# Six side tiles an l instead of three in a recommender kernel that gathers 200 x 16384 embedding rows

## Chip, core and metric

The kernel runs on one core of one Trainium2 chip. The metric is the device time of one execution in microseconds. Times are medians of runs; one further execution was taken with the hardware profiler, and all rows below are from it. Engines are named as in the profile: PE (matrix products; PEld is its loading of weights), DVE (vector), ACT (activations), POOL (GpSimd, here only the issuer of gathers) and SP (here only an issuer of copies). "SPq" and "ACTq" are the queues of instructions of these two engines that issue copies.

## What is computed

An attention unit over a history of L = 200 items for each of B = 16384 users, then a small head. Embeddings have D = 64 numbers (256 bytes a row).

```python
h = i_emb[hist]                                  # (200, 16384, 64)
itb = jnp.broadcast_to(it[None], h.shape)        # it = i_emb[item]
feat = jnp.concatenate([h, itb, h - itb, h * itb], axis=-1)
a = dice(feat @ au_W1 + au_b1, au_alpha, axis=1) # mean and variance over the 16384 users
w = a @ au_W2 + au_b2
cur = jnp.sum(w * h, axis=0)                     # sum over the history
z = jnp.concatenate([u, it, c, cur], axis=-1)    # u = u_emb[user], c = c_emb[cate]
z = dice(z @ W1 + b1, alpha1, axis=0)
z = dice(z @ W2 + b2, alpha2, axis=0)
return z @ W3 + b3
```

`dice(x)` normalizes x over the batch, takes a sigmoid p of it and gives x * (p + alpha * (1 - p)). Nearly all the work is in the rows `h`: 200 x 16384 of them, each read from a table in memory at a place that the input names.

## The kernel before

**Steps.** The 16384 users are 128 tiles of 128 rows (NT = 128). They are worked on in ND = 8 chunks c of TD = 16 tiles. One step k is one chunk of one l: k = 8 l + c, so an l is 8 steps and the whole history is 1600. A Python loop lays the steps out (`steps`); 90 l (LPB) are the body of a loop on the chip, and the last 20 l stand behind it. The order of instructions on each engine is that of the program text; every engine runs its own in order and waits for semaphores.

**Software pipeline of a step** (`step`, L435 on). In step k: `fetch(k)` lets POOL gather the rows of chunk k into `rows[k % 5]`; `hidden(k-2)` on ACT copies the products of chunk k-2 from `px` to `xs` with a bias; `ask_hist` issues row copies on SP (queue 0) and on ACT (queue 1); `gate(k-9)` is the sigmoid on ACT; ACT then issues what is left of its share; on DVE and PE `place(k-1)` and `turn(k-1)` bring chunk k-1 into the transposed layout and multiply it into `ph` and `px`; `measure(k-2)` gathers statistics; `product(k-1)` adds the last term to `px`; `weights(k-9)` and `weigh(k-9)` form the weighted sum of a chunk nine steps back into `curT`. Where chunk k-2 is the last of an l (k % 8 = 1), `measure` and `moments` come ahead of the rest, since the gates of that l need its mean and variance; in the program they stand directly behind `hidden`.

**Two ways to fetch rows.** Most tiles are gathered: POOL issues one indirect DMA for a tile of 128 rows (`gather`, L123), with indices that `load_hist_ids` put into `idx`. Some tiles are fetched *by address*: `SIDES` (L27) names the chunks whose last tile (n = 15) is such a side tile, NS = len(SIDES) of them an l. `fetch` leaves that tile out (`TD - has_side(k)`). Its rows are copied one by one, 256 bytes each, by plain DMAs on SP and ACT (`row_by_address`, L290). For this the indices of the NS x 128 side rows of an l are loaded onto one partition (`load_addresses`, by SP, two steps into the l before), multiplied by the row size on DVE (`scale_addresses`, two steps later), and loaded in groups into registers of the issuing engine (L326, the TENSOR_LOAD of the trace); each row is then one DMA with a register in its address (L294).

**Shares.** `ask_hist(k, queue, some)` asks in step c of an l for the c-th eighth of its side rows: NS x 128 / 8 = 48 rows. `shares` gives SP the first half of these and ACT the second (SPLIT = 0.5), and cuts each half into as few equal groups as hold at most LOAD = 28 rows, one load of addresses each: here one group of 24 rows on each queue. SP issues all its groups in a step at one place; ACT issues its first group ahead of the gate and any further groups behind it (`slice(0, 1)` and `slice(1, None)`).

**Side buffers.** Side tile m (counted over all l) is collected in `side[m % 6]` (BUFS = 6) and counted by the semaphore `landed[m % 6]`. In step k, `place(k-1)` has DVE wait for all 128 rows of the tile of chunk k-1, clear the semaphore and copy the tile into `rows` (L392). A buffer's next rows are asked for once that copy is done.

The head at the end gathers the user rows in the same way, with the side tiles of chunks 3 and 5 by address and the others by `side_ids` on POOL (L669 on).

Of the kernel before, what the change touches and what calls it, by code (L numbers as in the profile page):

```python
# [23 lines left out]
LAG = 9  # L24
XR = 8
IDX = 3
SIDES = (3, 5, 7)  # L27
BUFS = 6
LOAD = 28
SPLIT = 0.5  # L30
# [5 lines left out]
def din_kernel(  # L36
# [33 lines left out]
    ZB = Z1 - ZA  # L70
    NS = len(SIDES)
    serial = iter(range(10**6))
# [18 lines left out]
    def column(c, n):  # L91
        if c in SIDES and n == TD - 1:
            return NC + SIDES.index(c)
        return c * TD + n - sum(s < c for s in SIDES)

# [185 lines left out]
    def tiles_by_address(l):  # L281

        return l * NS, range(NS)
# [71 lines left out]
    def has_side(k):  # L355
        return k % ND in SIDES

# [26 lines left out]
    def place(k):  # L384
        if has_side(k):
            l, c = divmod(k, ND)
            first, tiles = tiles_by_address(l)
            place_tile(k, first + tiles.index(SIDES.index(c)))

    def place_tile(k, m):  # L390
        await_rows(m)
        nc.vector.tensor_copy(rows[k % ROWS][:, TD - 1], side[m % BUFS])  # L392
# [271 lines left out]
    with tc.manual_schedule():  # L664
# [1 line left out]
        U = addr[(L - BODY) % 3]  # L666
        first = -(-tiles_by_address(L - BODY)[0] // BUFS) * BUFS

        tiles = [SIDES.index(c) for c in (3, 5) if c in SIDES]  # L669
        weighed = {*range(-LAG, K - LAG), K, K + 1}  # L670
        for j in range(ND + 1):
            c = j - 1
# [128 lines left out]
```

## Time and profile before

| | us |
|---|---|
| median of 3 runs | 31650.93 |
| lowest to highest | 31650.28 to 31652.98 |
| the profiled execution | 31646.96 |
| its span, first to last instruction | 31645.1 |
| busy: POOL, PE, DVE, ACT | 23853.6, 20823.3, 15548.7, 3817.4 |

How to read it: busy time leaves out instructions that only an engine's sequencer runs, and the issue of plain DMAs is one of these, so SP has no busy time at all and ACT's contains its activations alone. Groups are given as "out<-in" with their count, busy time and mean, and behind the bar the time that the engine stood idle just before them and what ended it; "issue" there means that nothing the profile shows was waited for. In a timeline the columns are start, duration, engine, line, operation, and in brackets the idle time before it; rows on SPq and ACTq are issues of copies, merged where they follow one another. The granted clock of PE was 0.806 in this execution.

### The profile page before, as it was taken

What the parts mean: (1) busy time and instruction counts of PE and PEld (TensorE: products, weight loads), DVE (VectorE), ACT (ScalarE), POOL (GpSimd) and SP (SyncE); (2) the same over time, 40 slices, a digit from 0 to 9 for tenths busy, and PEclk for the clock granted to TensorE, in tenths of its full rate; (3) what the DMA queues carried; (4) which work ended last, traced back from release to release, by engine and by line L of the source; (5) the groups of instructions that cost most, each with busy time, mean ns of one, the idle gap of its engine ahead of it and who ended that gap; (6) DMA issues with size and microseconds to landing.
All of it is one profiled execution on the core that took longest, in us unless ns stands there. A gap on an engine that the chain in (4) does not pass through costs nothing.

```text
span 31645.1 us, 223489 instructions
## 1 busy us (share of the span) xinstructions
PE 20823.3 (66%) x39536; PEld 8584.9 (27%) x39536; DVE 15548.7 (49%) x21275; ACT 3817.4 (12%) x3322; POOL 23853.6 (75%) x25259
## 2 busy tenths in 40 slices
PE   6666666666666666666666666666666666666666
PEld 2222222222222222222222222222222222222222
DVE  5444444444444444444444444444444444444445
ACT  1111111111111111111111111111111111111111
POOL 7777777777777777777777777777777777777776
PEclk8888788887888888888788888887878788887888
DMA  2111111111111111111111111111111111111111
GB/s 44 28 28 28 28 28 28 28 28 28 28 28 28 28 28 28 28 28 28 28 28 28 28 28 28 28 28 28 28 28 28 28 28 28 28 28 28 28 28 30
DMA packets 1008142, 894.16 MB, mean 28 GB/s; under 512 B 597358, under 2 KB 597559, under 8 KB 1006695
## 3 DMA queue, kind: packets, MB, share of 16 engines
q0 software_dynamic: 808128, 829.14, 15.0%
q1 hardware_dynamic: 114362, 27.92, 0.4%
q10 hardware_dynamic: 84205, 22.70, 0.3%
q14 instruction: 1136, 9.31, 0.1%
q8 instruction: 311, 5.10, 0.1%
HBM read 873.48 MB, written 4.39 MB: 28 GB/s over the span
## 4 chain that ended last, share of the span: by engine, by line
POOL 30%; issue 11%; PE 6%; DMA 5%; DVE 2%; DVEq 0%; ACT 0%; POOLq 0%; ACTq 0%
POOL rows L124 30%; DMA rows<-in_L_rec_i_emb,idx 5%; PE px L154 3%; PE ph L154 2%; PE wb L154 2%; DVE hT L149 1%; DVE wb L373 1%; DVE curT L374 0%; DVE st L382 0%; DVEq L149 0%; DVE mv L418 0%; DVE rows L392 0%; DVE addrs L141 0%; POOLq L124 0%; PE pg L154 0%
## 5 line engine op out<-in xcount | busy, mean ns | idle before, releaser
L124 POOL DMA_INDIRECT rows<-in_L_rec_i_emb,idx x25000 | 23591.6, 944 | 7633.1 <-issue 7166.6
L154 PE MATMUL ph<-hT,unit 128*128 128x512 f32 x6404 | 5969.6, 1088 | 10697.5 <-DVE hT L149 10697.5
L373 DVE SCALAR_TENSOR_TENSOR wb<-wb,au_bias,hT 128x1024 f32<-128x1024 f32 x1609 | 2079.7, 1293 | 10748.4 <-PE wb L154 10748.4
L149 DVE STREAM_TRANSPOSE hT<-rows 64x512 f32<-64x512 f32 x6404 | 4518.5, 706 | 2971.8 <-DMA rows<-in_L_rec_i_emb,idx 2529.3
L154 PEld LDWEIGHTS ph<-hT,unit 128*128 128x128 f32 x6404 | 1796.1, 311 | 13756.3 <-DVE hT L149 13561.4
L154 PE MATMUL px<-hT,blk_h 128*128 128x512 f32 x6404 | 4065.3, 723 | 0.0
L377 ACT ACTIVATE xs<-px,au_bias 128x1024 f32<-128x1024 f32 x1602 | 1784.1, 1114 | 14492.6 <-PE wb L154 14492.5
L366 ACT ACTIVATE pg<-xs,sh,rs 128x1024 f32<-128x1024 f32 x1609 | 1943.3, 1208 | 12967.9 <-issue 10092.6
L154 PE MATMUL px<-itT,blk_i 128*128 128x512 f32 x6404 | 3382.0, 610 | 0.0
L154 PE MATMUL wb<-y,blk_p 128*128 128x512 f32 x6436 | 3291.1, 593 | 11.3 <-DVE y L369 11.3
L154 PE MATMUL wb<-xs,blk_x 128*128 128x512 f32 x6436 | 3289.2, 593 | 2.6 <-DVE curT L374 2.6
L154 PE MATMUL px<-hm,blk_m 128*128 128x512 f32 x6408 | 3011.3, 592 | 0.0
L412 DVE TENSOR_TENSOR hm<-ph,itT 128x1024 f32<-128x1024 f32 x1601 | 1960.4, 1224 | 1934.9 <-PE ph L154 1934.9
L154 PEld LDWEIGHTS px<-hT,blk_h 128*128 128x128 f32 x6404 | 1627.8, 254 | 2406.1 <-issue 2304.8
L382 DVE BATCH_NORM_STATS2 st<-xs 128x6 f32<-128x512 f32 x3204 | 2058.4, 684 | 44.5 <-ACT pg L366 0.3
L369 DVE TENSOR_TENSOR y<-pg,xs 128x1024 f32<-128x1024 f32 x1609 | 1955.7, 1215 | 85.0 <-ACT pg L366 82.9
L374 DVE TENSOR_TENSOR curT<-wb,curT 128x1024 f32<-128x1024 f32 x1609 | 1969.8, 1224 | 54.8
L154 PEld LDWEIGHTS px<-itT,blk_i 128*128 128x128 f32 x6404 | 1404.8, 219 | 2000.0 <-issue 2000.0
L154 PEld LDWEIGHTS wb<-y,blk_p 128*128 128x128 f32 x6436 | 1224.5, 190 | 1551.8 <-issue 1537.2
L154 PEld LDWEIGHTS wb<-xs,blk_x 128*128 128x128 f32 x6436 | 1224.3, 190 | 1541.4 <-issue 1538.0
L154 PEld LDWEIGHTS px<-hm,blk_m 128*128 128x128 f32 x6408 | 1219.0, 190 | 1531.4 <-issue 1524.2
L124 POOL DMA_INDIRECT rows<-in_L_rec_i_emb,ids x125 | 139.7, 1118 | 39.6 <-issue 37.2
(180 smaller groups left out, 1779.3 us busy)
## 6 DMA issues: line engine op xcount, KB each, us to landing
side<-in_L_rec_i_emb SPq DMA_DIRECT2D x38400, 0.2 KB
side<-in_L_rec_i_emb ACTq DMA_DIRECT2D x38400, 0.2 KB
rows<-in_L_rec_i_emb,idx POOLq DMA_INDIRECT x25000, 2.5
idx<-in_r_hist SPq DMA_DIRECT2D x200, 62.5 KB
hT<-cs ACTq DMA_DIRECT2D x16, 500.0 KB
ucT<-catT SPq DMA_DIRECT2D x8, 512.0 KB
side<-in_L_rec_u_emb SPq DMA_DIRECT2D x256, 0.2 KB
addrs<-in_r_hist SPq DMA_DIRECT2D x200, 1.5 KB
```

What stands on the lines that cost most here:

```text
L124: nc.gpsimd.indirect_dma_start(out=dst[:, n, :], out_offset=None, in_=table, in_offset=bass.IndirectOffsetOnAxis(ap=ids, axis=0),)
L149: nc.vector.transpose(by_tile(dst[ts(e, D)], i)[:, n], of[ts(i, D), n, ts(e, S)])
L154: nc.tensor.matmul(dst[:, ts(i, CH)], lhsT, rhs[:, ts(i, CH)], start=(first and j == 0), stop=(last and j == len(pairs) - 1), skip_group_c ...
L366: nc.scalar.activation(pg, xs[k % XR], AF.Sigmoid, bias=shifts[i], scale=rstds[i])
L369: nc.vector.tensor_mul(y, pg, xs[k % XR])
L373: nc.vector.scalar_tensor_tensor(wb, wb, au_bias2, hT[k % LAG], ALU.add, ALU.mult)
L374: nc.vector.tensor_add(curT[k % ND], wb, curT[k % ND])
L377: nc.scalar.activation(xs[k % XR], px, AF.Identity, bias=au_bias)
L382: nc.vector.bn_stats(stats[l % 3][:, 2 * c + i, :], xs[k % XR][:, ts(i, CH)])
L412: nc.vector.tensor_mul(hm, ph, itT[k % ND])
```

## The change

`SIDES` names six chunks in place of three. NS is 6, so an l has 122 gathered tiles and 6 side tiles (before: 125 and 3), 768 side rows instead of 384, and 96 of them a step. Each queue's share of a step is 48 rows; LOAD stays 28, so `shares` cuts it into two groups of 24. SP issues both at its place in the step, ACT one ahead of the gate and one behind it. The six side buffers hold one l instead of two. All tensors whose width is NS or NC change with it: `idx` and `ids` have 122 columns, `side_ids` 6, `addrs` 768 addresses for each of its three l.

```diff
-SIDES = (3, 5, 7)
+SIDES = (1, 3, 4, 5, 6, 7)
...
-        tiles = [SIDES.index(c) for c in (3, 5) if c in SIDES]
+        tiles = [SIDES.index(c) for c in (3, 5)]
```

The second edit gives the places of chunks 3 and 5 among the side tiles of the users: 0 and 1 before, 1 and 3 after. The head still fetches these two tiles by address and all other user tiles by POOL.

## The prediction

> **What bounds the kernel now.** I read the page first: engine shares, then the costliest groups.
>
> ```profile
> span 31645.1 us, 223489 instructions
> PE 20823.3 (66%) x39536; PEld 8584.9 (27%) x39536; DVE 15548.7 (49%) x21275; ACT 3817.4 (12%) x3322; POOL 23853.6 (75%) x25259
> L124 POOL DMA_INDIRECT rows<-in_L_rec_i_emb,idx x25000 | 23591.6, 944 | 7633.1 <-issue 7166.6
> side<-in_L_rec_i_emb SPq DMA_DIRECT2D x38400, 0.2 KB
> side<-in_L_rec_i_emb ACTq DMA_DIRECT2D x38400, 0.2 KB
> ```
>
> No engine is full by its busy share, but POOL's gathers fill the span together with the gap in front of each: (23591.6 + 7633.1) / 25000 = 1.249 us a gather, 125 gathers an l, 156.1 us an l, 200 l = 31225 of 31645 us. The rest is some 250 gathers of items and users and the head after them. The last two rows are what moves: 76800 row copies, half on SP, half on ACT. ACT's 12% leaves them out, because an issue isn't counted as busy.
>
> Then the waits, where 1.249 is confirmed and ACT's real load shows:
>
> ```profile
> ACT xs L377 <- PE wb L154: 14492.5, 1599, 15.7
> ACT pg L366 <- issue: 10092.6, 1242, 9.0
> POOL rows L124 <- issue: 7241.2, 23739, 0.3
> ACT pg L366 <- DVE sh L180: 1629.6, 201, 8.5
> DVE hT L149 <- DMA rows<-in_L_rec_i_emb,idx: 2529.3, 1181, 5.0
> ```
>
> POOL's gap is 0.3 us every time and waits for nothing: POOL runs without a stop. DVE waits for gathered rows 2529.3 us in all (12.6 an l), so the rest of the pipeline has spare time. The row of `pg` is the important one: before the gate, ACT is "idle" 10092.6 / 1242 = 8.13 us, each time "issue". That isn't spare time, it is the row copies being issued. The real spare time of ACT is the wait of `xs`, 14492.5 us.
>
> The timeline of ACT over one l shows how a step is built (hidden, 24 rows, gate, wait):
>
> ```profile
> 15032.23 1.11 ACT L377 ACTIVATE xs<-px,au_bias 128x1024 f32<-128x1024 f32 x1 [9.28 <-PE wb L154]
> 15033.94 7.31 ACTq L294 DMA_DIRECT2D side<-in_L_rec_i_emb  x24
> 15041.38 1.21 ACT L366 ACTIVATE pg<-xs,sh,rs 128x1024 f32<-128x1024 f32 x1 [8.04 <-DVE sh L180]
> 15055.80 1.11 ACT L377 ACTIVATE xs<-px,au_bias 128x1024 f32<-128x1024 f32 x1 [13.22 <-PE wb L154]
> 15057.54 7.29 ACTq L294 DMA_DIRECT2D side<-in_L_rec_i_emb  x24
> 15064.88 1.21 ACT L366 ACTIVATE pg<-xs,sh,rs 128x1024 f32<-128x1024 f32 x1 [7.96 <-issue]
> 15073.11 1.11 ACT L377 ACTIVATE xs<-px,au_bias 128x1024 f32<-128x1024 f32 x1 [7.03 <-PE wb L154]
> ...
> 15131.03 1.11 ACT L377 ACTIVATE xs<-px,au_bias 128x1024 f32<-128x1024 f32 x1 [9.97 <-PE wb L154]
> ...
> 15140.12 1.21 ACT L366 ACTIVATE pg<-xs,sh,rs 128x1024 f32<-128x1024 f32 x1 [7.97 <-issue]
> 15149.11 1.11 ACT L377 ACTIVATE xs<-px,au_bias 128x1024 f32<-128x1024 f32 x1 [7.79 <-PE wb L154]
> ...
> 15158.50 1.21 ACT L366 ACTIVATE pg<-xs,sh,rs 128x1024 f32<-128x1024 f32 x1 [8.27 <-issue]
> ```
>
> From the start of hidden to the start of the gate it is 9.08 us (15064.88 - 15055.80) to 9.39 us (15158.50 - 15149.11): 1.7 us until the first row, in which the 24 addresses are loaded while the activation runs, then 24 rows at 0.305 us. Call this a batch; its mean is 1.11 + 8.13 = 9.24 us by the row of the waits.
>
> **The change part by part.**
>
> *Removed:* three gathers an l on POOL, 600 x 1.249 = 749 us. POOL alone then needs 122 x 1.249 = 152.4 us an l, and the run 31647 - 749 = 30898 us. (The sum is made against the profiled execution, 31646.96 us, 4 us or 0.01% under the median of the three runs, 31650.93.)
>
> *Added on ACT:* a second batch of 24 rows in every step, behind the gate. It starts as the first does, with a load of addresses beside an activation (1.21 us instead of 1.11), so I price it like the first. Its ends in the rows above are 9.08 and 9.39; the mean, 9.24, includes the long stretches in which SP issues nothing (its waits are quoted below), and those go away. I take 9.30, a little above the mean, and keep 9.08 and 9.39 for the range. Next to be late is the next hidden, queued behind the second batch on ACT, and through it PE's px. So a step on ACT takes at least 2 x 9.30 = 18.60 us; the wait of `xs` hides the second batch only while steps are longer than that, and POOL's new mean step is 152.4 / 8 = 19.05. That would fit, were it not for one step of each l:
>
> ```profile
> 15188.89 1.11 ACT L377 ACTIVATE xs<-px,au_bias 128x1024 f32<-128x1024 f32 x1 [8.79 <-PE wb L154]
> 15210.87 1.11 ACT L377 ACTIVATE xs<-px,au_bias 128x1024 f32<-128x1024 f32 x1 [11.70 <-PE wb L154]
> ...
> 15500.21 1.11 ACT L377 ACTIVATE xs<-px,au_bias 128x1024 f32<-128x1024 f32 x1 [7.49 <-PE wb L154]
> 15523.62 1.11 ACT L377 ACTIVATE xs<-px,au_bias 128x1024 f32<-128x1024 f32 x1 [13.02 <-PE wb L154]
> ```
>
> The moments of an l are worked out on DVE between hidden and the next transposes, and PE's products come after these. So this step can't be shorter than it is: 15055.80 - 15032.23 = 23.57, 21.98 and 23.41 us here, mean 22.99. Today the following step catches up (15073.11 - 15055.80 = 17.3 us); with 18.60 us of ACT work it can't. ACT's shortest l is 22.99 + 7 x 18.60 = 153.2 us, against POOL's 152.4. ACT then sets the pace, by a little: 200 x (156.1 - 153.2) = 580 us saved, 31647 - 580 = 31067; I say 31060.
>
> The Trainium skill, page "DMA: Bandwidth & Descriptors", section "Issuing engines are not separate DMA queues", says that starting DMAs on several engines saves only the time of the sequencer that starts them, "usually small relative to the DMA itself". By that rule ACT's second batch would be nearly free and the time POOL's 30898; the 7.31 us for 24 copies of 256 B speak against it here.
>
> *Added on SP:* as much again.
>
> ```profile
> SPq L326 <- DVE rows L392: 15047.6, 198, 84.3
> SPq L132 <- DMA rows<-in_L_rec_i_emb,idx: 1283.4, 449, 8.0
> 15114.66 50.55 SPq L294 DMA_DIRECT2D side<-in_L_rec_i_emb  x139
> 15018.24 0.37 SPq L132 DMA_DIRECT2D idx<-in_r_hist  x1
> ```
>
> At full pace 139 rows with their loads of addresses take 50.55 us, so the 48 rows of a step take 48 x 50.55 / 139 = 17.5, an l 140 us, and the copies of `idx` and addresses (0.37 and the like) some 1 us more. That is below 152.4. SP stands still half the time, since it is up to two l ahead and waits for side tiles to be copied out (15047.6 us); the change spends that lead (six buffers then hold one l), not the path.
>
> *Added on DVE, and the small rest:*
>
> ```profile
> L392 DVE COPY rows<-side 128x64 f32<-128x64 f32 x603 | 128.1, 212 | 12.0 <-PEq L580 4.9 <-DMA rows<-in_L_rec_i_emb,idx 3.0
> L141 DVE TENSOR_SCALAR addrs<-addrs 1x384 int32<-1x384 int32 x201 | 75.1, 374 | 4.2
> ```
>
> Three copies more an l (0.21 each, plus a wait and a clear of the semaphore) and a scaling of 768 instead of 384 addresses (at most 0.37 more): about 1 us an l, hidden in DVE's 12.6 us of waiting for rows; without that cover it is 200 us. Head and end get some nine small copies, 0 to 5 us at 0.37 an issue. I take 0.
>
> **The wait on the last side tile.** Rows of the tile of c = 7 are asked for up to the end of step 7, now behind that step's gate, and DVE copies them in the next step:
>
> ```profile
> 14999.60 2.88 DVE L149 STREAM_TRANSPOSE hT<-rows 64x512 f32<-64x512 f32 x4 [3.75 <-DMA rows<-in_L_rec_i_emb,idx]
> 15012.64 1.11 ACT L377 ACTIVATE xs<-px,au_bias 128x1024 f32<-128x1024 f32 x1 [9.73 <-PE wb L154]
> 15014.83 1.23 DVE L374 TENSOR_TENSOR curT<-wb,curT 128x1024 f32<-128x1024 f32 x1
> 15015.97 0.18 DVE L392 COPY rows<-side 128x64 f32<-128x64 f32 x1
> ```
>
> The second batch must end by the next hidden (15012.64) and the copy comes 3.3 us after that, so a landing of up to 3.3 us is hidden. The queue behind the waiting copy is DVE's whole step. DVE and PE themselves take 15016.06 - 14999.60 = 16.5 us a step, under ACT's 18.6.
>
> **The rivals.**
> - *POOL stays the bound.* If a batch stays at 9.24 or under, ACT's l is 22.99 + 7 x 18.48 = 152.4 or less, POOL's figure: 30898 us. For it: the means agree to 0.1 us; against it: two limits so close disturb each other, and steps of ACT vary. Chance 0.30; the skill's rule above would lead here as well.
> - *The side tile is awaited.* With a landing of 5.0 us (the longest wait of DVE for rows in the table) the copy in step 0 comes at hidden + 5.0, the weighing ends 16.7 us later at 21.7, and the measuring of the step with the moments, due at 18.6 + 1.1 = 19.7, is 2.0 us late each l: 31060 + 400 = 31460. Against it: the lead of 3.3 us. Chance 0.05.
> - *Slower than before: the two queues slow one another.* ACT and SP now issue at the same time almost always, where SP stood half the time. From 22.99 + 14b > 156.1, b > 9.51 us a batch, ACT's l is longer than POOL's is today; that is 0.27 us on the mean batch, 11 ns a row. At 9.65 us (the longest batch, 9.0 + 1.1 = 10.1, is beyond it) it is 158.1 us an l, 31647 + 400 = 32050. For it: the 9.39 of 15149.11 lies in SP's run from 15114.66 to 15165.21; against it: so does the 9.09 of 15131.03. Chance 0.10.
> - *Nothing to be measured*, b about 9.5: 0.03.
>
> **How the numbers follow.** ACT just above POOL: 0.52, with its own range 30960 (9.26) to 31350 (22.99 + 14 x 9.39 = 154.5 gives 31327). The predicted time is this case's 31060. Low 30885 takes in POOL's case, high 31350 the dearest batch seen; about 0.18 is left out. A measurement tells some 0.2% (63 us) from no change: faster 0.87 (0.52 + 0.30 + 0.05), within it 0.03, slower 0.10.
>
> **What would show it.** In the profile after: 24400 gathers at 1.249; two groups of 24 rows in each step of ACT, 9.3 us from activation to the start of the next one; the waits of `xs` down from 14492.5 to about a thousand us, nearly all in the step of the moments; POOL with some hundred us of waits for `rows` to come free if ACT leads, with none if POOL does; SP's wait for DVE down to 2000 to 3000 us. It would be wrong if ACT's batches take 9.5 us or more, if DVE waits at L392, or if steps other than that of the moments exceed 19 us.

## The result, and the profile after

| | us |
|---|---|
| before, median of 4 runs | 31651.43 |
| after, median of 4 runs | 33150.12 (33129.22 to 33179.11) |
| ratio after to before | 1.0474, 95% interval 1.0456 to 1.0492 |
| the profiled execution after | 33179.11 |

The change makes the kernel 4.7% slower; 31060 with a range of 30885 to 31350 was predicted. The page of the changed kernel shows the span, the busy times, the queues of the DMAs (packets, MB, share of the time of 16 DMA engines; q0 holds the gathers), the gathers and the copies out of the side tiles.

```profile
span 33177.3 us, 305303 instructions
PE 20799.5 (63%) x39536; PEld 8515.3 (26%) x39536; DVE 15729.4 (47%) x21875; ACT 3816.8 (12%) x3322; POOL 23292.1 (70%) x24659
q0 software_dynamic: 788928, 809.44, 14.8%
q1 hardware_dynamic: 192026, 37.90, 3.8%
q10 hardware_dynamic: 161869, 32.68, 3.3%
L124 POOL DMA_INDIRECT rows<-in_L_rec_i_emb,idx x24400 | 23030.3, 944 | 9721.0 <-issue 6147.0
L392 DVE COPY rows<-side 128x64 f32<-128x64 f32 x1203 | 253.4, 211 | 1598.0 <-DMA side<-in_L_rec_i_emb 1583.1
```

The 600 gathers are gone, but each of those left now takes (23030.3 + 9721.0) / 24400 = 1.342 us with the gap in front of it, where it was 1.249. 122 x 1.342 = 163.8 us an l, against 156.1 before: POOL still fills the span, at a slower pace. The 0.944 us of the instruction itself haven't changed; the gap has. The queues of SP (q1) and ACT (q10) in the same list before were:

```profile
q1 hardware_dynamic: 114362, 27.92, 0.4%
q10 hardware_dynamic: 84205, 22.70, 0.3%
```

There are less than twice as many packets, but their share of the DMA engines' time has grown about tenfold. Share x 16 engines x span / packets gives a mean of 0.004 x 16 x 31645 / 114362 = 18 ns a packet on q1 before and 0.038 x 16 x 33177 / 192026 = 105 ns after. So the packets of the row copies are themselves slower.

The waits of the changed kernel say what the gap of POOL is:

```profile
ACT xs L377 <- PE wb L154: 11433.4, 1059, 16.5
ACT pg L366 <- issue: 10749.7, 1310, 10.6
POOL rows L124 <- issue: 6221.4, 19504, 3.9
POOL rows L124 <- DMA rows<-in_L_rec_i_emb,idx: 3521.8, 5054, 2.6
DVE rows L392 <- DMA side<-in_L_rec_i_emb: 1583.1, 199, 13.3
```

5054 gathers wait for DMAs of earlier gathers, 3521.8 us in all. Before, the same row was there at the length of POOL's usual gap:

```profile
POOL rows L124 <- DMA rows<-in_L_rec_i_emb,idx: 336.0, 1102, 0.3
```

At 0.305 us a gather, 5054 gaps would be 1541 us, so these waits hold 1980 of the 2270 us by which POOL's gaps have grown. DVE waits 199 times, once an l, for a side tile, 8.0 us each. The first batch of ACT is 10749.7 / 1310 + 1.11 = 9.32 us, and ACT still has 11433.4 us of waiting for PE: ACT isn't what sets the pace. A piece of the timeline at step 0 of an l shows both waits:

```profile
15247.37 1.11 ACT L377 ACTIVATE xs<-px,au_bias 128x1024 f32<-128x1024 f32 x1 [11.34 <-PE wb L154]
15249.10 7.39 ACTq L294 DMA_DIRECT2D side<-in_L_rec_i_emb  x24
15252.33 0.94 POOL L124 DMA_INDIRECT rows<-in_L_rec_i_emb,idx  x1 [0.47 <-DMA rows<-in_L_rec_i_emb,idx]
15254.16 0.94 POOL L124 DMA_INDIRECT rows<-in_L_rec_i_emb,idx  x1 [0.89 <-DMA rows<-in_L_rec_i_emb,idx]
15256.19 0.94 POOL L124 DMA_INDIRECT rows<-in_L_rec_i_emb,idx  x1 [1.09 <-DMA rows<-in_L_rec_i_emb,idx]
15256.33 0.20 DVE L392 COPY rows<-side 128x64 f32<-128x64 f32 x1 [5.56 <-DMA side<-in_L_rec_i_emb]
15257.55 2.88 DVE L149 STREAM_TRANSPOSE hT<-rows 64x512 f32<-64x512 f32 x4 [1.02 <-DMA rows<-in_L_rec_i_emb,idx]
```

All rows of that side tile had been issued by the hidden of 15247.37 (ACT's last ones by 15244.40, SP's earlier), and the last of them lands some 9 us after it, at 15256.33. Right behind the copy DVE waits another 1.02 us for the gathered rows of the same chunk.

### The profile page after: what moved, and what is told of

Same layout as the page of the kernel before. It is cut to its first block, busy times and chain, and to the rows that moved or that the text cites. A ratio compares the mean times of both kernels' runs of the same rounds, so it can differ in the third digit from the quotient of the medians.

```text
span 33177.3 us, 305303 instructions
## 1 busy us (share of the span) xinstructions
PE 20799.5 (63%) x39536; PEld 8515.3 (26%) x39536; DVE 15729.4 (47%) x21875; ACT 3816.8 (12%) x3322; POOL 23292.1 (70%) x24659
## 3 DMA queue, kind: packets, MB, share of 16 engines
q0 software_dynamic: 788928, 809.44, 14.8%
q1 hardware_dynamic: 192026, 37.90, 3.8%
## 4 chain that ended last, share of the span: by engine, by line
DMA 27%; POOL 17%; issue 7%; ACTq 1%; PE 1%; DVE 1%; ACT 0%; DVEq 0%; POOLq 0%
DMA rows<-in_L_rec_i_emb,idx 27%; POOL rows L124 17%; ACTq L294 1%; PE px L154 0%; PE ph L154 0%; PE wb L154 0%; DVE hT L149 0%; DMA side<-in_L_rec_i_emb 0%; ACT pg L366 0%; ACT xs L377 0%; ACTq L326 0%; DVE wb L373 0%; DMA rows<-in_L_rec_u_emb,ids 0%; DVE hm L412 0%; DVE curT L374 0%
## 5 line engine op out<-in xcount | busy, mean ns | idle before, releaser
L124 POOL DMA_INDIRECT rows<-in_L_rec_i_emb,idx x24400 | 23030.3, 944 | 9721.0 <-issue 6147.0
L149 DVE STREAM_TRANSPOSE hT<-rows 64x512 f32<-64x512 f32 x6404 | 4517.7, 705 | 2637.5 <-DMA rows<-in_L_rec_i_emb,idx 2332.8
L377 ACT ACTIVATE xs<-px,au_bias 128x1024 f32<-128x1024 f32 x1602 | 1783.8, 1114 | 15901.3 <-PE wb L154 11433.4
L366 ACT ACTIVATE pg<-xs,sh,rs 128x1024 f32<-128x1024 f32 x1609 | 1943.0, 1208 | 13099.3 <-issue 10749.7
L392 DVE COPY rows<-side 128x64 f32<-128x64 f32 x1203 | 253.4, 211 | 1598.0 <-DMA side<-in_L_rec_i_emb 1583.1
```

The costliest lines, as they stand in the source:

```text
L124: nc.gpsimd.indirect_dma_start(out=dst[:, n, :], out_offset=None, in_=table, in_offset=bass.IndirectOffsetOnAxis(ap=ids, axis=0),)
L149: nc.vector.transpose(by_tile(dst[ts(e, D)], i)[:, n], of[ts(i, D), n, ts(e, S)])
L366: nc.scalar.activation(pg, xs[k % XR], AF.Sigmoid, bias=shifts[i], scale=rstds[i])
L377: nc.scalar.activation(xs[k % XR], px, AF.Identity, bias=au_bias)
```

## The experiments

Two theories stood at the start. E: the row copies and the gathers get in each other's way in the DMA engines, and beyond some rate (first taken as 4.8 copies a us, 96 in a step of 20 us) both land late. R: what costs is only that the last tile's second group of rows stands behind the gate. To compare runs by an l, I take off what lies outside the 1600 steps, 31647 - 31225 = 422 us in the kernel before, and divide by 200. The changed kernel's l is (33179 - 422) / 200 = 163.8 us: 768 copies at 4.69 a us.

**Four and five side tiles** (`e1_four`, `e2_five`).

```diff
-SIDES = (3, 5, 7)
+SIDES = (3, 5, 6, 7)
```
```diff
-SIDES = (3, 5, 7)
+SIDES = (3, 4, 5, 6, 7)
```

> Four side tiles an l (chunks 3, 5, 6, 7), else the kernel before; 64 row copies a step, two groups of 16 on ACT. Theory E (all row copies pass through one DMA engine that manages about 4.8 rows a us beside the gathers): 64 rows in 19.4 us are 3.3 a us, below the limit, so POOL sets the pace: 31647 - 200 x 1.249 = 31397, no long wait of DVE at the side tiles. Rival R (what costs is only that ACT's second group stands behind the gate, so that the last tile is asked for too late): the wait at the last tile of each l is there too, some us an l, 31600 to 32400.

> Five side tiles an l (chunks 3 to 7), else the kernel before; 80 row copies a step. E: 80 rows in 19.2 us are 4.2 a us, near but under 4.8: between POOL's pace, 31647 - 400 x 1.249 = 31147, and some hundred us above it from late rows, 31150 to 31600. R: the wait at the last tile as with six, about 8 us an l above POOL's pace, 32500 or more.

Measured: 31407 us with four (ratio 0.9924, 0.9907 to 0.9941) and 31157 with five (0.9845, 0.9829 to 0.9861). Both are POOL's pace within 10 us. With five, ACT also has a second group of rows behind the gate, and the last tile is that of chunk 7 as well; R falls. Five is the fastest complete kernel of this study. Its queue and gathers:

```profile
q1 hardware_dynamic: 166138, 34.57, 0.6%
L124 POOL DMA_INDIRECT rows<-in_L_rec_i_emb,idx x24600 | 23216.2, 944 | 7518.7 <-issue 7147.0
L392 DVE COPY rows<-side 128x64 f32<-128x64 f32 x1003 | 210.2, 210 | 16.3 <-PEq L580 7.4
```

With 80 copies a step a packet takes 18 ns, as before, a gather 1.249 us, and no side tile is waited for. Between 80 and 96 everything turns.

**Rows of half the bytes** (`e3_half_rows`).

```diff
-                        side[m % BUFS].bitcast(U8)[p : p + 1],
-                        flat[ds(a, ROW)].rearrange("(o d) -> o d", o=1),
+                        side[m % BUFS].bitcast(U8)[p : p + 1, : ROW // 2],
+                        flat[ds(a, ROW // 2)].rearrange("(o d) -> o d", o=1),
```

> The changed kernel with row copies of 128 bytes instead of 256 (the second half of each side row is left out), the same number of copies. E, with a limit in packets: no change, 33150 within 100. E, with a limit in bytes: the engine is half as loaded and the time falls to ACT's or POOL's pace, 30900 to 31100. R says nothing of the bytes: 33150.

Measured: 33147 us, no change, as for a limit in packets. But the profile isn't that of the changed kernel:

```profile
q1 hardware_dynamic: 192026, 28.04, 0.9%
ACT pg L366 <- issue: 11707.3, 1325, 10.6
ACT xs L377 <- issue: 4470.9, 484, 10.6
POOL rows L124 <- DVE hT L149: 1718.2, 331, 9.4
```

Here a packet takes 25 ns, while the first batch on ACT has grown to 11707.3 / 1325 + 1.11 = 9.95 us, and ACT's waits for PE have fallen from 11433.4 to 4286.0 us: ACT now leads. The median issue of a row on ACT is the same (274 ns, 273 in the changed kernel), so a part of the issues takes longer. The copies are held back where they are issued more than where they land. The time is the same and the way to it is not; I can't say that the two have one cause.

**A step of lead** (`e4_lead`). Each share of rows is asked for one step earlier.

```diff
+        ahead[0] = n * ND
+        for q in range(2):
+            ask_hist(0, q, slice(None))
         for k in range(n * ND):
...
-            ask_hist(k, 0, slice(None))
-            ask_hist(k, 1, slice(0, 1))
+            ask_hist(k + 1, 0, slice(None))
+            ask_hist(k + 1, 1, slice(0, 1))
...
-            ask_hist(k, 1, slice(1, None))
+            ask_hist(k + 1, 1, slice(1, None))
...
+        if k == ahead[0]:
+            return
         l, s = divmod(k, ND)
```

> The changed kernel with each share of rows asked for one step earlier (the first share of each of the three blocks of steps at its start). R: the last tile has a whole step more, the wait is gone and ACT's pace is left, 31060 to 31200. E: the wait at the side tile goes, but the engine still has 96 rows a step at 4.8 a us, 20 us a step, so 200 x 160 + 450 = 32400, 32000 to 32700, with POOL still waiting for DMAs.

Measured: 32960 us (1.0415, 1.0398 to 1.0433), 260 us above E's range: 768 copies in 162.7 us an l are 4.72 a us, not 4.8. Its waits:

```profile
DVE hT L149 <- DMA rows<-in_L_rec_i_emb,idx: 3621.4, 1108, 13.0
POOL rows L124 <- DMA rows<-in_L_rec_i_emb,idx: 3189.5, 4526, 2.8
```

The wait of DVE for side tiles, 1583 us in the changed kernel, is gone from the list, and only 190 us came of it. DVE waits for gathered rows in its place (3621.4 instead of 2332.8), and POOL for its DMAs as before. So the late side tile is a symptom that would cost little; the late gathers are the cost.

**Six tiles, the rows of one not copied** (`e5_one_left_out`).

```diff
         first, tiles = tiles_by_address(l)
+        first, tiles = first + 1, tiles[1:]
```

> The changed kernel, but the rows of the first side tile of each l (chunk 1) are not copied: 122 gathers and 6 tiles stay, 80 copies a step instead of 96. E (a limit near 4.7 copies a us for both queues together): 80 in 19.05 us are 4.2 a us, so POOL's pace is left, 30890 to 30960. If something else of the six tiles costs (buffers, the wait on the last tile, more copies on DVE): well above, 31500 or more.

Measured: 30928 us (0.9773, 0.9756 to 0.9789). With the same six tiles, 122 gathers and buffers, taking away a sixth of the copies takes away the whole loss, and POOL's pace of the prediction (30898) is there within 30 us. Its packets and gathers are as they were with three tiles, 18 ns and 1.250 us:

```profile
q1 hardware_dynamic: 166426, 34.57, 0.6%
L124 POOL DMA_INDIRECT rows<-in_L_rec_i_emb,idx x24400 | 23043.8, 944 | 7458.3 <-issue 7158.2
```

**The copies alone** (`e6_copies_alone`). POOL gathers as many tiles as before the change.

```diff
-        for n in range(TD - has_side(k)):
-            j = column(c, n)
+        for n in range(TD - (has_side(k) and c not in (1, 4, 6))):
+            j = column(c, min(n, TD - 1 - has_side(k)))
```

> The changed kernel, but POOL gathers 125 tiles an l as before: in chunks 1, 4 and 6 it also gathers into the side tile's place (rows that are then overwritten). 96 copies a step stay. E: 768 copies an l at 4.7 a us are 163.4 us, above POOL's 156.1, so the gathers do not matter: 33050 to 33300. The model of the prediction (ACT 153.2, POOL 156.1): 31650 to 31750.

Measured: 33187 us (1.0489, 1.0471 to 1.0506), 163.8 us an l, what the changed kernel takes with 122 gathers.

```profile
L124 POOL DMA_INDIRECT rows<-in_L_rec_i_emb,idx x25000 | 23597.2, 944 | 9157.4 <-issue 6680.6
```

A gather takes (23597.2 + 9157.4) / 25000 = 1.310 us here, less than the 1.342 with 122 of them. What stays the same is 4.69 copies a us, with 122 gathers and with 125: POOL's pace follows the copies. (DVE also waits 1596.9 us here before the copies out of the side tiles, for the gathers into their place; only this edit makes that wait, and no run separates it.)

**Gathers of half the bytes** (`e7_half_gathers`) **and half as many gathers** (`e13_half_the_gathers`).

```diff
-            out=dst[:, n, :],
-            in_=table,
+            out=dst[:, n, : D // 2],
+            in_=table.rearrange("v (h d) -> (v h) d", h=2),
```
```diff
-        for n in range(TD - has_side(k)):
+        for n in range(TD // 2):
```

> The changed kernel, but each gathered row is 128 bytes (the second half of every gathered row is left out, and the first is of another place): POOL's instructions and the 96 copies a step stay, the gathers move half the bytes. E, with copies slowed by sharing a DMA engine with the gathers' data: the limit rises above 5.2 a us and the time falls to 30900 to 31500. E, with a limit of the copies by themselves: unchanged, 33000 to 33250.

> The changed kernel with 8 gathers a step instead of 15 or 16 (the other tiles of each chunk are left out); 96 copies a step stay. POOL then needs only 80 us an l. E, with a limit of the copies by themselves: 768 / 4.7 = 163.4 us an l, 33000 to 33200. E, with copies slowed by the gathers on a shared DMA engine: the limit rises, ACT's pace of the prediction shows, 153.2 us an l, 30900 to 31150.

Measured: 33103 us with half the bytes, no change to speak of (33150); 31197 us with half the gathers, (31197 - 422) / 200 = 153.9 us an l. The queues of the two runs, and behind those of `e13` three of its waits:

```profile
q0 software_dynamic: 788928, 405.51, 11.0%
q1 hardware_dynamic: 192026, 37.90, 3.7%
```
```profile
q0 software_dynamic: 417728, 428.59, 7.3%
q1 hardware_dynamic: 192026, 37.90, 0.8%
ACT pg L366 <- issue: 10972.7, 1330, 9.4
POOL rows L124 <- DVE hT L149: 15029.1, 1577, 19.6
DVE rows L392 <- DMA side<-in_L_rec_i_emb: 1073.8, 200, 9.9
```

`e7` alone would fit a limit of the copies by themselves; `e13` rules out one at 4.7 a us, as 768 copies in 153.9 us are 4.99. Both move about the same megabytes on q0, 405 and 429. With 788928 packets of gathers the row copies' packets take 102 ns, with 417728 they take 21. So it is the number of the gathers, or of their packets (`e13` halves both), that slows the copies, and not their bytes. In `e13` POOL waits 15029.1 us for buffers to come free and ACT leads: with half the gathers, 96 copies a step cost about what the prediction had summed for ACT, 153.2 us an l, 153.9 measured (47 us above the range expected of the run). The last side tile of an l is still waited for, 5.4 us each time.

**Half a tile left out** (`e8_half_a_tile`, `e10_half_a_tile_2`, `e12_half_a_tile_24`).

```diff
-        runs = shares(len(tiles) * P // ND, s, SPLIT)[queue]
+        runs = shares((len(tiles) * P - D) // ND, s, SPLIT)[queue]
+        runs = [(r0 + D, end + D) for r0, end in runs]
...
+                    counts[m] = counts.get(m, 0) + 1
...
-            fence = nc.vector.wait_ge(landed[m % BUFS], 16 * P)
+            fence = nc.vector.wait_ge(landed[m % BUFS], 16 * counts.pop(m))
```

and, in `e12_half_a_tile_24` alone,

```diff
-            at = [r0 + (end - r0) * i // loads for i in range(loads + 1)]
+            at = [r0, r0 + 24, end] if end - r0 == 44 else [r0, end]
```

> The changed kernel, but 64 of the 128 rows of the first side tile of each l are not copied: 88 copies a step. E: at POOL's pace 88 in 19.05 us are 4.62 a us, just under 4.7, so 30900 to 31200, with some late rows. If the limit lies lower than that (between 4.2, which ran freely, and 4.6): 31200 to 32000, with waits of POOL for DMAs as in the changed kernel.

> The kernel of e8 once more, since the kernel before itself took 41804 us on that chip. 88 copies a step. E: at POOL's pace 4.62 a us, just under 4.7: 30900 to 31200. If the limit lies between 4.2 and 4.6: 31200 to 32000, with waits of POOL for DMAs as in the changed kernel.

> 88 copies a step as in e10, but each queue's 44 rows in groups of 24 and 20, so that no load of addresses starts off a multiple of 16 bytes. If e10's loss is its loads of 22 addresses (1.9 and 5.0 us), it is gone here. E then: POOL's pace with 4.62 copies a us, 30900 to 31200; with a limit between 4.2 and 4.6, 31200 to 32000.

`e8` ran on a chip on which the kernel before took 41804 us; it took 47528 there and says nothing of the limit. `e10` took 33930 us beside 31648 for the kernel before, more than the changed kernel with its 96 copies, and for a reason of its own, which its timeline of ACT shows:

```profile
15006.73 6.85 ACTq L295 DMA_DIRECT2D side<-in_L_rec_i_emb  x22
15013.63 1.21 ACT L369 ACTIVATE pg<-xs,sh,rs 128x1024 f32<-128x1024 f32 x1 [7.75 <-DVE hT L149]
15018.68 6.84 ACTq L295 DMA_DIRECT2D side<-in_L_rec_i_emb  x22
```

From the gate to the first row of the second group it is 5.05 us, not 1.8: the load of 22 addresses that lies between them takes that long. The edit had moved the second group of each queue 8 bytes off a multiple of 16 bytes; the first group, also of 22 but on such a multiple, has its first row 1.95 us after hidden (15028.14 - 15026.19). With groups of 24 and 20 that start on one, `e12` took 31009 us (0.9798, 0.9781 to 0.9814), POOL's pace and 110 us, 704 copies in (31009 - 422) / 200 = 152.9 us, 4.60 a us:

```profile
q1 hardware_dynamic: 179226, 36.24, 3.0%
POOL rows L124 <- DMA rows<-in_L_rec_i_emb,idx: 245.3, 603, 1.5
DVE rows L395 <- DMA side<-in_L_rec_i_emb: 338.3, 193, 10.1
```

The slow packets are there already (83 ns), but the copies nearly keep up: DVE waits 338.3 us for side tiles, not 1583.1. So the edge lies between 88 and 96 copies a step beside POOL's full stream of gathers.

**A row in two pieces** (`e9_two_pieces`, `e11_two_pieces_2`), with five side tiles.

```diff
-    side = [make(f"side{i}", P, D) for i in range(BUFS)]
+    side = [make(f"side{i}", P, 2, D) for i in range(BUFS)]
...
-                        side[m % BUFS].bitcast(U8)[p : p + 1],
-                        flat[ds(a, ROW)].rearrange("(o d) -> o d", o=1),
+                        side[m % BUFS].bitcast(U8)[p : p + 1, :, : ROW // 2],
+                        flat[ds(a, ROW)].rearrange("(o k d) -> o k d", o=1, k=2),
```

> The kernel with five side tiles, each row copied as two pieces of 128 bytes to two places of a wider side tile in one DMA: 80 DMAs but 160 pieces a step. If the limit counts DMAs, or packets of one DMA engine while the two pieces go to two engines: unchanged, 31157 within 60. If it counts pieces in one place for all of them (160 in 19.2 us are 8.3 a us, over 4.7): far slower, 40000 to 56000.

> The kernel of e9 once more, for the same reason: five side tiles, each row copied as two pieces in one DMA. A limit that counts DMAs, or packets of each of two engines: 31157 within 60. A limit that counts pieces in one place: 40000 to 56000. If the two pieces take longer to issue (on the other chip a copy took 0.66 us instead of 0.30): ACT needs 2 x (1.7 + 20 x 0.66) = 30 us a step, 48000.

Measured: 65238 us on the slow chip, 52563 us on another one. Two of the alternatives allow that time, a limit that counts pieces in one place and a slower issue. The timeline of ACT in the second run speaks for the issue:

```profile
15006.00 1.21 ACT L366 ACTIVATE pg<-xs,sh,rs 128x1024 f32<-128x1024 f32 x1 [15.07 <-issue]
15008.09 14.09 ACTq L294 DMA_DIRECT2D side<-in_L_rec_i_emb  x20
15022.28 1.11 ACT L377 ACTIVATE xs<-px,au_bias 128x1024 f32<-128x1024 f32 x1 [15.08 <-issue]
```

20 rows take 14.09 us, 0.70 each where a row in one piece takes 0.305, so a step needs 2 x 16.3 us on ACT, and 8 x 32.6 = 261 us an l are what was measured. The median issue itself has grown (697 ns on ACT, 273 with five tiles in one piece), on SP as well (675, 252), and a packet of q1 takes 14 ns. But 160 pieces in 32.6 us are 4.9 a us, close to the limit of the single rows, so a limit in pieces that holds back the issue isn't excluded. The run doesn't tell whether the limit is one DMA engine's or lies in one place for all of them.

## Why the prediction was wrong

- *What bounds the kernel* was right for the kernel before. After the change POOL's gathers still fill the span, but now they wait for DMAs. The step that failed is the first term of the sum, "600 x 1.249 = 749 us. POOL alone then needs 122 x 1.249 = 152.4 us an l". The 600 gathers were saved, but 1.249 was taken as a constant of POOL. It became 1.342, and 24400 x 0.093 = 2270 us more is what turned a gain of 749 into a loss of about 1500. The wait behind it is in the trace of before, 1102 times, but no longer than POOL's 0.3 us of "issue", so nothing there told its size at a higher rate of copies; "0.3 us every time and waits for nothing" passed over it.
- *Added on ACT*: right in the main. 9.30 us a batch was taken; the first one measured 9.32 (9.36 in `e13`, and the second 4826.3 / 588 + 1.21 = 9.42 there, by the row of `xs` waiting for "issue"). The sum of 153.2 us an l came out as 153.9 in `e13`, the run in which ACT leads. That it came so close is in part luck: averaged over that run, the step of the moments took 21.9 us and not 22.99 (so it could be shorter), and the other seven 18.8 and not 18.60. ACT's bound was real, but the late DMAs were a tighter one.
- *Added on SP*, and *on DVE*: no run shows them on the path. SP still waited 2882.5 us for side tiles to be copied out, inside the 2000 to 3000 that were forecast.
- *What wasn't in the sum*: the copies were costed by their issue alone, 0.305 us of a queue each, and their transfers at nothing. Doubling them put 96 instead of 48 on the DMAs that the gathers also run on. `e6` shows that they cost the whole loss without a gather removed, `e5` that the loss goes with a sixth of them, `e13` that it also goes with half the gathers. The Trainium skill has the sentence that I needed in the section that I cited for another one ("DMA: Bandwidth & Descriptors", "Issuing engines are not separate DMA queues"): DMAs started by ACT, SP and POOL "will ultimately run on the same 16 DMA engines and interleave with each other". The trace is in keeping with it, with a packet of q1 at 18 ns below the edge and 105 beyond it, though it doesn't show at which DMA engine.
- *The wait on the last side tile*: it did appear, larger than the rival had it (the copy came 9.0 us after hidden, not 5.0), but `e4` shows that it isn't the cost.
- *The rival on the other side*, two queues that slow one another's issue, had the sign and neither the size (32050) nor the mechanism: the first batch stayed at 9.32 us, and the transfers slowed. In `e3`, with 128-byte rows, the issue does slow; whether the two queues slow one another there isn't shown.
- *What would show it*: "24400 gathers at 1.249" failed; the batch of 9.3 us held; the wait of `xs`, forecast at about a thousand us, stayed at 11433.4, since ACT didn't lead. Two of its signs of being wrong came true: DVE waited at L392, and the mean step of an l was 163.8 / 8 = 20.5 us, so that more steps than that of the moments exceeded 19.

What stays open: why 83 to 105 ns a packet of the copies, while the gathers' own packets (q0) hardly change from before to after, 0.150 x 16 x 31645 / 808128 = 94 ns and 0.148 x 16 x 33177 / 788928 = 100 ns, though the gathers come late; and at which place of the DMA path the gathers' packets and the row copies meet (one DMA engine, or something common to all). The two-piece copies were to tell, and their slower issue hid it. Why rows of 128 bytes come to the same time by way of a slower issue is open too.

## What to carry to other kernels

Moving work from a busy issuer to queues with time to spare has two prices, the issue and the transfer: cost small DMAs also by their number beside all the other DMAs in flight (here halving the gathers' bytes changed nothing, halving their number did), and not by the queue's idle time alone. A pace per instruction that looks like a constant (1.249 us, waiting for nothing) holds only as long as what it feeds keeps up; ask what would make it wait. And this limit had an edge: against POOL's 30898, 80 copies a step cost 30 us, 88 cost 110 and 96 cost 2250, so try the sizes between before giving up the idea.

## What the runs showed of the hardware that I had not expected

- Beside gathers of 128 rows every 1.249 us, a core's two queues copied rows of 256 bytes freely at 4.2 a us and nearly freely at 4.60, but didn't pass 4.72 (`e4`, 768 in 162.7 us); with half the gathers, 4.99.
- Loading addresses into registers depended on where they start: on ACT 24 took 1.7 us (changed kernel) and 20 took 1.4, both on a multiple of 16 bytes, but 22 took 1.9 to 5.2 us (median 3.5): about 1.9 where a group starts on such a multiple and about 5 where it starts 8 bytes off. The instructions of that line in `e2_five` (20) and in `e10` (22), as min/median/max in ns:

```profile
L326 ACTq TENSOR_LOAD <-addrs x3200: 1417/1437/1661, 192.5 to 30906.2; - x189
```
```profile
L327 ACTq TENSOR_LOAD <-addrs x3200: 1857/3505/5179, 192.9 to 33671.4; - x189
```

- On one chip the kernel before took 41804 us instead of 31650. There 47 rows of `e8` on SP took 30.61 us with their loads, 0.65 each; the same kernel elsewhere (`e10`) had 125 in 55.67, 0.45 each. The median issue on SP was the same, 252 ns, and the longest 1574 against 629, so a part of the issues was slow and not every one. Why is open, and the ratios of this chip aren't comparable with those of the other chips.

```profile
14999.41 30.61 SPq L295 DMA_DIRECT2D side<-in_L_rec_i_emb  x47
```
```profile
14999.97 55.67 SPq L295 DMA_DIRECT2D side<-in_L_rec_i_emb  x125
```
